# Attention after a recurrent layer, fp32: the row maxima of a unit are turned earlier, and two engines read a step's scores in opposite order

## The chip, the cores and the metric

One core of a Trainium2 chip. Its engines each work through a queue of their own in order: TensorE (PE in the profile, with its weight loads as PEld), VectorE (DVE), ScalarE (ACT), GpSimd (POOL) and SyncE (SP, for DMAs). The metric is the device time of one execution in microseconds (us). The kernel before takes 1719.53 us, the median of three runs (1718.27 to 1722.62).

## The reference

The input `x` is 2 x 2048 x 256, all in fp32. A layer norm and a tanh recurrence come first; their result is added to `x`. Then comes an attention layer with 8 heads of width 64, over 2048 queries and keys in each of the two batches, whose values and output go through gated experts:

```python
q = (x @ Wq).reshape(b, t, h, dh).transpose(0, 2, 1, 3)
k = (x @ Wk).reshape(b, t, h, dh).transpose(0, 2, 1, 3)
v = jnp.einsum('bthe,btek->bhtk', wv, xv)          # wv: top 2 of 5 gates, xv: 5 experts
scores = jnp.einsum('bhid,bhjd->bhij', q * scale, k)
probs = jax.nn.softmax(scores, axis=-1)
attn = jnp.einsum('bhij,bhjd->bihd', probs, v)
out = jnp.einsum('bthe,bthk,ekd->btd', mask_o, attn, Wo)
```

The softmax is what the change is about: each query needs the largest of its 2048 scores before any exponential can be taken.

## The kernel before

The first 180 us (recurrence, norms, the first batch's gates and experts) are not touched. The attention is 16 heads (2 batches x 8) of four **units** each: a unit is one head and one block of 512 queries, 64 units in all. Scores are held turned, keys on the partitions. A unit has eight **pairs** of key blocks; a pair is 2 x 128 keys by 512 queries, a tile of 128 x 1024. The main loop (L864) takes one **step** T at a time, with two new pairs in each, so a unit takes four steps: T % 4 = 0 brings pairs 0 and 1, and T % 4 = 3 brings pairs 6 and 7. I call them steps 0 to 3. `manual_schedule` keeps the order in which the code issues; there is no planner.

For a new pair `scores` (L497) issues matmuls into a PSUM tile `s`, of which there are two (`ps_s`, bufs=2), so a pair's tile is written again one step later, when all of its readers are done. `stage` (L512) has ScalarE copy it to SBUF, into `p`. `largest` (L517) has VectorE take the running maximum `m` (L525); pair 0 is not read for this, since pair 1 is compared with pair 0's copy. The last pair of the unit is handled in halves (L528 to L531), which gives `mm`, one maximum per partition and query. Where ScalarE and VectorE read the same PSUM tile, the framework orders the two reads as the code has them.

In step 0 of the next unit these maxima are turned: `turn_max` (L534) transposes `mm` on TensorE into `pm`, `reduce_max` (L541) has VectorE take the maximum along the row (`mq`, L543), and `spread_max` (L545) broadcasts and transposes it back into `pt` (L553), of which ScalarE makes a copy `top` in SBUF (L556). In step 1 pairs 0 and 1 have the maximum subtracted on VectorE, from `pt` in PSUM (`subtract`, L558 and L563); pairs 2 to 7 follow in steps 2, 3 and 0 on GpSimd, from `top`. ScalarE takes the exponential in place (L566). A step later `products` (L568) multiplies by the values into `o`; `fold` (L585) adds pairs with GpSimd DMAs and `sums` (L590) forms the denominators `d` with matmuls, in odd steps.

Other work hangs in two tables of steps: `before` runs ahead of a step's products, `behind` at its end. In step 0 `behind` holds `close` of an older unit, registered ahead of the newer unit's `spread_max`. `close` transposes that unit's result into `po` on TensorE (`weigh`, L629), and has VectorE form the denominators and gates (`den` L631, L635, L638) and the masked product `pro` (L642). At step 2 `take` (L608) reads `o` with ScalarE and then VectorE (`os`, L613); at step 3 `take_sums` does so for `d` (L619, L620). `keys` and `queries` of the next head stand in step 2 of three units of four, and in step 3 of one. `mix` (L488, `xq`) and `mix_sum` (L494) form the values in steps 2 and 3. Small PSUM tiles (`pm`, `pt`, `po`, `pk`, `pq`, `pv`, `pgl`, `py`, `pz`, `mh`) share two buffers (`misc`, L401).

Of the kernel before, what the change touches and what calls it, by code (L numbers as in the profile page):

```python
# [20 lines left out]
def rnn_then_switchhead_kernel(  # L21
# [16 lines left out]
    B, T, D = x.shape  # L38
# [20 lines left out]
    for c in range(NCH):  # L59
        t = rconst.tile([P, B, D], F32, tag=f"x{c}", name=f"x{c}")  # L60
# [258 lines left out]
    with tc.tile_pool(name="rnn", bufs=2) as rp, tc.tile_pool(  # L319
# [7 lines left out]
        for g in range(2):  # L327
            mv = rp.tile([P, GC, 2], F32, tag="mv", name=f"mvb{g}")
            for k in range(GC):
                c = g * GC + k  # L330
# [10 lines left out]
            for k in range(0, GC, 2):  # L341
                c = g * GC + k
# [25 lines left out]
            for k in range(GC):  # L368
                c = g * GC + k
# [22 lines left out]
    U_T = NCH // 4  # L392
# [8 lines left out]
    def misc(shape, nm):  # L401
        return ps_m.tile(shape, F32, tag="m", name=nm)
# [3 lines left out]
    NT = len(units) * U_T  # L406
    k_of, v_of, q_of, xq_of, y_of = {}, {}, {}, {}, {}
    ring, m_of, mm_of, mx_of, top_of, o_of, den_of = {}, {}, {}, {}, {}, {}, {}
    HC = NCH // 2
# [24 lines left out]
    def queries(i, part):  # L434

        b, h = heads[i]
        pq = misc([P, QB], f"pq{i}_{part}")
        for kc in range(KC):
            for o in range(2):
                n = 2 * part + o  # L440
                for g in range(0, DH, 32):
                    at_col = o * DH + g
                    nc.tensor.matmul(  # L443
                        pq[at_col : at_col + 32, :],
                        lhsT=wq[:, kc, h * DH + g : h * DH + g + 32],
                        rhs=xn2T[:, kc, b, n * QB : (n + 1) * QB],
                        start=kc == 0,
                        stop=kc == KC - 1,
                        tile_position=(0, at_col),
                    )  # L450
        q = ap.tile([P, QB], F32, tag="q", name=f"q{i}_{part}")
        qs = ap.tile([P, QB], F32, tag="qs", name=f"qs{i}_{part}")
        nc.scalar.mul(q, pq, SCALE)
        nc.sync.dma_start(out=qs[0:DH, :], in_=q[DH:P, :])
        nc.sync.dma_start(out=qs[DH:P, :], in_=q[0:DH, :])
        q_of[i, 2 * part] = (q, qs)
        q_of[i, 2 * part + 1] = (qs, q)
# [39 lines left out]
    def scores(t):  # L497
        i, n = units[t // HC]
        c = t % HC
        ss = ps_s.tile([P, 2, QB], F32, tag="s", name=f"s{t}")  # L500
        for o in range(2):
            half = slice(o * DH, (o + 1) * DH)
            nc.tensor.matmul(  # L503
                ss[:, o, :],
                lhsT=k_of[i][half, c, :],
                rhs=q_of[i, n][o][half, :],
                start=True,
                stop=True,
            )
        return ss  # L510

    def stage(t, ss):  # L512
        p = ap.tile([P, 2, QB], F32, tag=f"p{t % 2}", bufs=RING[t % 2], name=f"p{t}")
        nc.scalar.copy(p, ss)  # L514
        ring[t] = p

    def largest(t, ss):  # L517
        u, c = t // HC, t % HC
        if c == 0:
            return  # L520
        if c == 1:
            m_of[u] = ap.tile([P, 2, QB], F32, tag="mx", bufs=1, name=f"m{u}")
        m = m_of[u]
        if c < HC - 1:
            nc.vector.tensor_tensor(m, ss, ring[t - 1] if c == 1 else m, ALU.max)  # L525
            return
        half = misc([P, QB], f"mh{u}")
        nc.vector.tensor_tensor(half, ss[:, 0, :], m[:, 0, :], ALU.max)  # L528
        nc.vector.tensor_tensor(m[:, 1, :], ss[:, 1, :], m[:, 1, :], ALU.max)
        mm_of[u] = ap.tile([P, QB], F32, tag="mm", bufs=1, name=f"mm{u}")  # L530
        nc.vector.tensor_tensor(mm_of[u], half, m[:, 1, :], ALU.max)  # L531
        m_of.pop(u)

    def turn_max(u):  # L534
        pm = misc([P, QS, P], f"pm{u}")
        mm = mm_of.pop(u)
        for s in range(QS):
            nc.tensor.transpose(pm[:, s, :], mm[:, s * P : (s + 1) * P], ident)
        mx_of[u] = (pm, ap.tile([P, QS], F32, tag="mq", name=f"mq{u}"))

    def reduce_max(u):  # L541
        pm, mq = mx_of[u]
        nc.vector.tensor_reduce(mq, pm, AX.X, ALU.max)  # L543
# [14 lines left out]
    def subtract(t):  # L558
        u, c = t // HC, t % HC
        p = ring[t]  # L560
        last = u == len(units) - 1 and c % 2 == 0
        eng, top = (nc.vector, top_of[u][0]) if c < 2 or last else (nc.gpsimd, top_of[u][1])
        eng.tensor_tensor(p, p, top.unsqueeze(1).to_broadcast([P, 2, QB]), ALU.subtract)  # L563

    def exponential(t):
        nc.scalar.activation(ring[t], ring[t], AF.Exp)  # L566
# [18 lines left out]
    def fold(t):  # L585


        nc.gpsimd.dma_start(out=ring[t], in_=ring.pop(t + 1), accum_op=ALU.add)  # L588
# [19 lines left out]
    def take(u):  # L608

        o = o_of.pop(u)  # L610
        os = ap.tile([P, QB], F32, tag="os", bufs=1, name=f"os{u}")
        nc.scalar.copy(os[0:DH, :], o[0:DH, :])
        nc.vector.tensor_tensor(os[0:DH, :], o[DH:P, :], os[0:DH, :], ALU.add)  # L613
        o_of["s", u] = os
# [159 lines left out]
        late["c"].pop(0)()  # L774


    before, behind = {}, {}

    def at(table, T, f, *a):
        table.setdefault(T, []).append(lambda: f(*a))  # L780
# [5 lines left out]
    for i, (b, h) in enumerate(heads):  # L786
# [8 lines left out]
        for part in range(4):  # L795
            if i == 0:
                T = LAG - 3 + part
# [3 lines left out]
            else:  # L801
                T = max(T0 + U_T * (part - 3) + 2, LAG + 2)
# [6 lines left out]
    for b in range(1, B):  # L809

        T0 = (b - 1) * H * H_T + 2 * LAG + 3
        for c in range(NCH):
            T = T0 + c // 2 * U_T
# [6 lines left out]
        for c in range(NCH):  # L820
            T = T0 + 2 * c
# [12 lines left out]
    for u, (i, n) in enumerate(units):  # L834
        b, h = heads[i]
        T1 = (u + 1) * U_T
        at(before, T1, turn_max, u)
        at(before, T1, reduce_max, u)
        at(behind, T1, spread_max, u)
        outs = [(b, n * QS + s) for s in range(QS)]  # L840
        if u == len(units) - 1:

            outs = [(b, c) for c in range(n * QS - QS, n * QS + QS)]
            todo = [(turn_out, *outs[0])]
            for k, o in enumerate(outs):
                todo += [(turn_out, *x) for x in outs[k + 1 : k + 2]] + [(project_out, *o)]
            at(behind, T1 + LAG - 1, fetch_y, u)
            for x in todo[:3] + [(take_sums, u), (close_last, u)] + todo[3:]:
                at(behind, T1 + LAG, *x)
            continue  # L850
        at(behind, T1 + LAG + 1, take_sums, u)
        at(behind, T1 + LAG + 2, close, u)
        at(behind, T1 + LAG + 3, gather, u)
        if h == H - 1:
            at(behind, T1 + LAG, fetch_y, u)
            if u < len(units) - 2:
                for s in range(QS):
                    at(behind, T1 + LAG + 4 + s, turn_out, *outs[s])
                    at(behind, T1 + LAG + 5 + s, project_out, *outs[s])

    with tc.manual_schedule():
        queries(0, 0)
        keys(0, 0)
        for T in range(NT + LAG + 1):  # L864
            new = [t for t in (2 * T, 2 * T + 1) if T < NT]
            sub = [t for t in (2 * (T - LAG + 1), 2 * (T - LAG + 1) + 1) if 0 <= t < 2 * NT]
            old = [t for t in (2 * (T - LAG), 2 * (T - LAG) + 1) if 0 <= t < 2 * NT]
            u_old = (T - LAG) // U_T - 1
            done = (T - LAG) % U_T == 0 and 0 <= u_old < len(units)
            if done:  # L870
                take(u_old)
            if sub and sub[0] % HC == 0:
                subtract(sub[0])
            if old:
                exponential(old[1])
            for t in new:
                ss = scores(t)
                stage(t, ss)
                largest(t, ss)
            if sub and sub[0] % HC:  # L880
                subtract(sub[0])
            k = T - LAG
            if 0 < k < NT - U_T + 1:
                fold(2 * (k - 1))
            if sub:
                subtract(sub[1])
            for f in before.pop(T, []):
                f()
            for t in old:
                products(t)  # L890
            if 3 <= k and k % 2 and k - 3 < NT - U_T:
                t = 2 * (k - 3)
                sums(t, t + 2, t % HC == 0, t % HC != 0)
            if NT - 2 <= k < NT:

                t0 = 2 * (NT - U_T)
                for t in range(t0, t0 + 4, 2) if k == NT - 2 else ():
                    sums(t, t + 1, t == t0, False)
                sums(2 * k, 2 * k + 1, False, k == NT - 1)
            if sub:  # L900
                exponential(sub[0])
            for f in behind.pop(T, []):
                f()
        assert not before and not behind


# [44 lines left out]
```

## Time and profile before

| | |
|---|---|
| median of three runs | 1719.53 us |
| the profiled execution | 1725.14 us, span 1723.4 us |
| mean granted clock of TensorE | 0.982 |
| busy: PE, DVE, ACT, POOL | 91%, 76%, 71%, 73% |
| attention, from the first to the last score matmul | 178.6 to 1649.7 us |
| 1100 to 1640 us: busy PE, PEld, DVE, ACT, POOL | 512.5, 167.6, 457.5, 435.8, 464.3 of 540 us |
| pages' costliest groups: PE `s` (L503) | 2 x 526 us, 632 ns each |
| DVE maximum (L525) | 391.8 + 78.4 us, 1224 ns each |
| ACT copy (L514), exponential (L566) | 494.4 and 540.0 us, 1015 and 1066 ns each |
| POOL and DVE subtraction (L563) | 2996 and 1210 ns each |

A group row of the profile gives busy time, the mean duration of one instruction, and the idle time of the engine before it with what ended it. A wait row reads "who, line, waited for whom, line: us in total, times, longest". In a timeline row the first two numbers are start and duration, and x2 or x16 means that so many instructions are merged. Matmuls overlap, so their start-to-start distance counts, not their duration.

### The profile page before, as it was taken

The page shows a single profiled execution, that of the slowest core. Times are in us where ns is not written, and L with a number is a line of the kernel's source. Part 1 is how long each engine was busy: PE and PEld are TensorE (multiplying, and loading weights), DVE is VectorE, ACT ScalarE, POOL GpSimd, SP SyncE. Part 2 cuts the span into 40 slices and gives each one's busy share as a digit, 9 for nine tenths or more (in the row PEclk, how much of TensorE's full clock was granted, in tenths as well). Part 3 has the DMA queues.
Part 4 walks back from the last instruction along what each step waited for, and adds up shares of the span by engine and source line. Part 5 has one row for each costly group of instructions (what it writes and reads, how often), then busy time and mean ns, then how long its engine had stood idle before and what let it go on. Part 6 is the DMA issues. An engine that isn't in the chain of part 4 may idle for free.

```text
span 1723.4 us, 27125 instructions
## 1 busy us (share of the span) xinstructions
PE 1571.2 (91%) x10338; PEld 623.2 (36%) x10338; DVE 1312.7 (76%) x1861; ACT 1229.2 (71%) x1609; POOL 1264.5 (73%) x832
## 2 busy tenths in 40 slices
PE   6978689999989999999999999999999999999986
PEld 5976223232223333333323343333333333333234
DVE  5464588989887876678887668888888888888752
ACT  3642468787777887678887667787878787878861
POOL 3001667888778987679998757888888888888870
PEclk9998889999999999999999999999999999999999
DMA  4003157788777877678887656788888888888752
GB/s 152 1 34 116 54 132 175 174 181 171 153 155 159 165 159 162 153 154 161 166 174 161 153 133 164 167 160 169 162 170 161 169 162 169 162 168 182 150 121 80
DMA packets 88918, 254.74 MB, mean 148 GB/s; under 512 B 12176, under 2 KB 33488, under 8 KB 88784
## 3 DMA queue, kind: packets, MB, share of 16 engines
q0 software_dynamic: 43200, 163.60, 52.0%
q1 hardware_dynamic: 43952, 88.76, 16.1%
q8 instruction: 83, 1.36, 0.3%
q10 hardware_dynamic: 1632, 0.61, 0.1%
q14 instruction: 51, 0.42, 0.1%
HBM read 62.08 MB, written 50.33 MB: 65 GB/s over the span
## 4 chain that ended last, share of the span: by engine, by line
PE 49%; DVE 23%; ACT 11%; issue 5%; DMA 4%; POOL 1%; SPq 0%; ACTq 0%; DVEq 0%; POOLq 0%
PE s L503 20%; PE o L576 13%; DVE m L525 11%; ACT p L514 7%; PE d L597 4%; PE pq L443 3%; DVE p L563 3%; PE pt L553 2%; PE pk L424 2%; DVE mq L543 2%; DVE xq L488 2%; ACT p L566 2%; DVE v L494 1%; DMA p<-p 1%; PE pz L715 1%
## 5 line engine op out<-in xcount | busy, mean ns | idle before, releaser
L563 POOL TENSOR_TENSOR p<-p,top 128x1024 f32<-128x1024 f32 x381 | 1049.4, 2996 | 19.7 <-ACT top L556 19.7
L566 ACT ACTIVATE p<-p 128x1024 f32<-128x1024 f32 x512 | 540.0, 1066 | 79.2 <-DVE p L563 77.2
L503 PE MATMUL s<-qs,k 64*128 64x512 f32 x1024 | 525.9, 632 | 18.7 <-DVE m L525 18.4
L503 PE MATMUL s<-q,k 64*128 64x512 f32 x1024 | 526.1, 632 | 10.8 <-DVE m L525 10.1
L514 ACT COPY p<-s 128x1024 f32<-128x1024 f32 x512 | 494.4, 1015 | 20.7 <-PE s L503 17.4
L576 PE MATMUL o<-p,v 128*32 128x512 f32 x4096 | 493.1, 598 | 10.8 <-DVE os L613 7.5
L525 DVE TENSOR_TENSOR m<-s,m 128x1024 f32<-128x1024 f32 x320 | 391.8, 1224 | 136.5 <-ACT p L514 119.4
L588 POOL DMA_DIRECT2D p<-p x252 | 320.1, 1270 | 82.5 <-ACT p L514 35.5
L503 PEld LDWEIGHTS s<-qs,k 64*128 64x128 f32 x1024 | 173.0, 189 | 162.4 <-DVE m L525 86.3
L576 PEld LDWEIGHTS o<-p,v 128*32 128x32 f32 x4096 | 112.7, 109 | 315.6 <-issue 191.0
L503 PEld LDWEIGHTS s<-q,k 64*128 64x128 f32 x1024 | 172.9, 189 | 148.4 <-DVE m L525 70.1
L563 DVE TENSOR_TENSOR p<-p,pt 128x1024 f32<-128x1024 f32 x131 | 158.5, 1210 | 0.1
L525 DVE TENSOR_TENSOR m<-s,p 128x1024 f32<-128x1024 f32 x64 | 78.4, 1224 | 83.9 <-ACT p L514 83.5
L597 PE MATMUL d<-p,ones 128*32 128x512 f32 x1040 | 136.2, 592 | 0.7 <-DMA p<-p 0.7
L684 POOL DMA_DIRECT2D yd<-pro x48 | 42.3, 882 | 123.6 <-DVE pro L642 121.7
L556 ACT COPY top<-pt 128x512 f32<-128x512 f32 x64 | 37.5, 586 | 107.8 <-PE pt L553 107.8
L488 DVE TENSOR_TENSOR xq<-xq,wp 128x1280 f32<-128x1280 f32 x64 | 95.1, 1487 | 10.0 <-DMA xq<-xvd 8.0
L642 DVE TENSOR_TENSOR pro<-po,mr 128x1280 f32<-128x1280 f32 (+1 forms) x67 | 95.9, 1431 | 2.7
L494 DVE TENSOR_REDUCE v<-xq 128x256 f32<-128x1280 f32 x64 | 94.5, 1476 | 0.1
L156 POOL TENSOR_SCALAR xn<-x,mb,zb 128x256 f32<-128x256 f32 x8 | 5.2, 656 | 107.8 <-DVE zb L146 90.9
L553 PE MATMUL pt<-ident,mq 128*128 128x128 f32 x256 | 42.3, 289 | 43.1 <-DVE mq L543 42.4
L443 PE MATMUL pq<-xn2T,wq 128*32 128x512 f32 x512 | 61.6, 598 | 5.7 <-DVE xq L488 4.6
(139 smaller groups left out, 1544.7 us busy)
## 6 DMA issues: line engine op xcount, KB each, us to landing
p<-p POOLq DMA_DIRECT2D x252, 512.0 KB, 5.7
xq<-xvd SPq DMA_DIRECT2D x64, 640.0 KB, 6.2
yd<-pro POOLq DMA_DIRECT2D x48, 640.0 KB, 6.8
qs<-q SPq DMA_DIRECT2D x64, 128.0 KB, 2.3
yd<-pro SPq DMA_DIRECT2D x8, 640.0 KB, 3.8
y<-yd SPq DMA_DIRECT2D x8, 640.0 KB, 6.1
x<-in_x SPq DMA_DIRECT2D x16, 256.0 KB, 5.5
x1d<-x SPq DMA_DIRECT2D x16, 256.0 KB, 2.0
```

The lines of the kernel that those rows point to most:

```text
L443: nc.tensor.matmul(pq[at_col : at_col + 32, :], lhsT=wq[:, kc, h * DH + g : h * DH + g + 32], rhs=xn2T[:, kc, b, n * QB : (n + 1) * QB], s ...
L488: nc.vector.tensor_tensor(xq, xq, wp.unsqueeze(2).to_broadcast([P, 4, DH, E]), ALU.mult)
L494: nc.vector.tensor_reduce(v_of[i][:, 4 * part : 4 * part + 4, :], xq, AX.X, ALU.add)
L503: nc.tensor.matmul(ss[:, o, :], lhsT=k_of[i][half, c, :], rhs=q_of[i, n][o][half, :], start=True, stop=True,)
L514: nc.scalar.copy(p, ss)
L525: nc.vector.tensor_tensor(m, ss, ring[t - 1] if c == 1 else m, ALU.max)
L563: eng.tensor_tensor(p, p, top.unsqueeze(1).to_broadcast([P, 2, QB]), ALU.subtract)
L566: nc.scalar.activation(ring[t], ring[t], AF.Exp)
L576: nc.tensor.matmul(o_of[u][at_col : at_col + 32, :], lhsT=v_of[i][:, 2 * c + o, g : g + 32], rhs=ring[t][:, o, :], start=c == 0, stop=c == ...
L588: nc.gpsimd.dma_start(out=ring[t], in_=ring.pop(t + 1), accum_op=ALU.add)
L597: nc.tensor.matmul(den_of[u][32 * g : 32 * (g + 1), :], lhsT=ones32, rhs=ring[(t, t1)[g // 2]][:, g % 2, :], start=first, stop=last, tile_ ...
L642: nc.vector.tensor_tensor(dst, po[:, s : s + n, 0:DH].unsqueeze(2).to_broadcast([P, n, E, DH]), mr[:, s : s + n].unsqueeze(3).to_broadcast ...
```

## The change

Three things change in the order in which a step issues; no instruction is added or removed.

In steps 0, `turn_max` and `reduce_max` are issued ahead of the step's own maximum instead of in the table `before`, and `spread_max` goes to a table of its own, `first_behind`, which runs ahead of all that is in `behind`. In steps 1 to 3 the two engines begin with different pairs: ScalarE copies the first pair and then the second, VectorE takes the maximum of the second pair and then of the first; the half-wise handling moves from the last pair to the last but one. In step 1 the second subtraction on VectorE stands between the two maxima, where it was behind both.

```diff
     def largest(t, ss):
         u, c = t // HC, t % HC
-        if c == 0:
-            return
...
-        if c < HC - 1:
+        if c != HC - 2:
             nc.vector.tensor_tensor(m, ss, ring[t - 1] if c == 1 else m, ALU.max)
             return
...
-        at(before, T1, turn_max, u)
-        at(before, T1, reduce_max, u)
-        at(behind, T1, spread_max, u)
+        at(first_behind, T1, spread_max, u)
...
-            if sub and sub[0] % HC == 0:
+            fresh = sub and sub[0] % HC == 0
...
+            if fresh:
                 subtract(sub[0])
             if old:
                 exponential(old[1])
-            for t in new:
-                ss = scores(t)
-                stage(t, ss)
-                largest(t, ss)
-            if sub and sub[0] % HC:
+
+            ss = [scores(t) for t in new]
+            if new:
+                stage(new[0], ss[0])
+            if T % U_T == 0:
+                if new:
+                    stage(new[1], ss[1])
+                if 0 < T <= NT:
+                    turn_max(T // U_T - 1)
+                    reduce_max(T // U_T - 1)
+                if new:
+                    largest(new[1], ss[1])
+            elif new:
+                largest(new[1], ss[1])
+                stage(new[1], ss[1])
+            if fresh:
+                subtract(sub[1])
+            if T % U_T and new:
+                largest(new[0], ss[0])
+            if sub and not fresh:
                 subtract(sub[0])
             k = T - LAG
             if 0 < k < NT - U_T + 1:
                 fold(2 * (k - 1))
-            if sub:
+            if sub and not fresh:
                 subtract(sub[1])
...
-            for f in behind.pop(T, []):
+            for f in first_behind.pop(T, []) + behind.pop(T, []):
                 f()
```

More of the change, by code (lines that the diff above doesn't have):

```diff
@@ L774, in gates_go_on @@
         late["c"].pop(0)()
-    before, behind = {}, {}
+    before, first_behind, behind = {}, {}, {}
     def at(table, T, f, *a):
@@ L864, in rnn_then_switchhead_kernel @@
         for T in range(NT + LAG + 1):
-            new = [t for t in (2 * T, 2 * T + 1) if T < NT]
+            new = (2 * T, 2 * T + 1) if T < NT else ()
             sub = [t for t in (2 * (T - LAG + 1), 2 * (T - LAG + 1) + 1) if 0 <= t < 2 * NT]
@@ L901, in rnn_then_switchhead_kernel @@
                 exponential(sub[0])
-            for f in behind.pop(T, []):
+            for f in first_behind.pop(T, []) + behind.pop(T, []):
                 f()
-        assert not before and not behind
+        assert not before and not behind and not first_behind
 def kernel(
```

## The prediction

> **What bounds the kernel now.** I read the page first, then the granted clock (0.982, so nothing is explained by it), then the waits of 1100 to 1640 us, where the kernel only repeats itself, and last the timelines of one unit there.
>
> ```profile
> PE 1571.2 (91%) x10338; PEld 623.2 (36%) x10338; DVE 1312.7 (76%) x1861; ACT 1229.2 (71%) x1609; POOL 1264.5 (73%) x832
> ```
>
> TensorE is busy 91% of the span, in 1100 to 1640 even 512.5 of 540 us. The 27.5 us that are left there, some 5%, are nearly all in four waits (us in total, times, longest):
>
> ```profile
> PEld s L503 <- DVE m L525: 69.0, 100, 1.5
> DVE m L525 <- ACT p L514: 63.9, 52, 2.4
> ...
> ACT p L566 <- DVE p L563: 35.6, 25, 1.4
> ...
> PE pt L553 <- DVE mq L543: 16.8, 26, 0.7
> ...
> PE s L503 <- DVE m L525: 5.6, 14, 0.6
> ...
> PE o L576 <- DVE os L613: 3.0, 7, 0.4
> ...
> PE pq L443 <- DVE xq L488: 2.4, 6, 0.4
> ```
>
> The PE rows, 16.8 + 5.6 + 3.0 + 2.4 = 27.8 us, are idle time of TensorE; the PEld rows are weight loads, which run beside matmuls and cost nothing by themselves. The wait that comes once in every unit is `pt` on `mq`, 0.65 us. DVE's wait for ACT's copy, and ACT's for DVE's subtraction, lie on engines with idle time. Here is that place on TensorE (start, duration):
>
> ```profile
> 1312.90 0.65 PE L538 MATMUL pm<-ident,mm 128*128 128x128 f32 x4
> 1313.48 1.92 PE L576 MATMUL o<-p,v 128*32 128x512 f32 x16
> 1315.34 0.66 PE L629 MATMUL po<-ident,os 128*128 128x128 f32 x4
> 1316.64 0.65 PE L553 MATMUL pt<-ident,mq 128*128 128x128 f32 x4 [0.65 <-DVE mq L543]
> 1317.22 0.69 PE L503 MATMUL s<-q,k 64*128 64x512 f32 x1
> ...
> 1321.85 0.69 PE L503 MATMUL s<-q,k 64*128 64x512 f32 x1
> ```
>
> and on VectorE:
>
> ```profile
> 1314.77 1.23 DVE L525 TENSOR_TENSOR m<-s,p 128x1024 f32<-128x1024 f32 x1 [0.59 <-ACT p L514]
> 1315.91 0.68 DVE L543 TENSOR_REDUCE mq<-pm 128x4 f32<-128x512 f32 x1
> 1316.50 0.16 DVE L631 TENSOR_REDUCE den<-po 128x4 f32<-128x8 f32 x1
> ...
> 1317.13 1.49 DVE L642 TENSOR_TENSOR pro<-po,mr 128x1280 f32<-128x1280 f32 x1
> 1318.54 1.21 DVE L563 TENSOR_TENSOR p<-p,pt 128x1024 f32<-128x1024 f32 x1
> 1319.81 2.56 DVE L525 TENSOR_TENSOR m<-s,m 128x1024 f32<-128x1024 f32 x2
> 1322.28 1.21 DVE L563 TENSOR_TENSOR p<-p,pt 128x1024 f32<-128x1024 f32 x1
> ```
>
> I count a step from the first matmul of its scores. Step 0 (T divisible by 4) starts at 1310.98, step 1 at 1317.22, step 2 at 1321.85, then 1327.34 and 1331.97: lengths 6.24, 4.63, 5.49, 4.63, together 20.99 us per unit. The reader is to see two things. TensorE has no gap but the 0.65. And in step 1 VectorE is the engine with a backlog: it comes to step 1 with `pro` and two subtractions to do beside the two maxima. It still frees the first pair's buffer in time: the first maximum ends 1.235 us after 1319.81, at S1 + 3.82 (S1 is the start of step 1), and TensorE comes back to that buffer at S1 + 4.63. The cover is 0.8 us.
>
> **Part 1: turned maxima ahead.** `mq` no longer stands behind the maximum at 1314.77, which waits for ScalarE. VectorE is done with `os` (L620) at 1314.18 and `pm` at 1313.55, so `mq` runs from about 1314.2 to 1314.9; `o` ends its issue at 1315.34, where `pt` now follows at once. The 0.65 us goes. The maximum starts at 1314.9 rather than 1314.77, which nobody waits for. Step 0 on TensorE is then 1.92 (scores) + 0.58 (`pm`) + 1.86 (`o`) + 0.58 (`pt`) + about 0.66 (`po`, by its own row) = 5.60, against 6.24. But `spread_max` now stands in a list that runs ahead of `close`, so `pt` is ahead of `po`, and `po` is the last thing in step 0. It ends about 0.08 after S1, and `den` follows 0.04 later (units at 995 to 1030 us show 0.04 from `po` to `den`): `den` at S1 + 0.12, where it was at S1 - 0.72. So what VectorE still has to do comes later against S1, not earlier. ScalarE's `top` comes 0.6 us earlier, which POOL's subtractions don't wait for here.
>
> **Part 2: different pairs first, and the second subtraction between the maxima.** In step 1 VectorE's queue was `pro`, subtract, max of pair one, max of pair two, subtract. Now it is `pro`, subtract, max of pair two, subtract, max of pair one. From start to start, by the rows above: `den` to `pro` 0.63, `pro` to subtract 1.41, subtract to max 1.27, max to subtract 1.24, subtract to max 1.27, and 1.23 for the last: 7.05 us. From S1 + 0.12 the first pair's buffer comes free at S1 + 7.17, and TensorE needs about 0.05 after a release (at 1347.79 after a maximum ending at 1347.74): step 2 starts at **S1 + 7.22, not at S1 + 4.63**. Nothing else on TensorE can fill this: the scores are the first matmuls of step 2, and both steps' products stand behind or are done. This is the new wait, +2.59 us. All its instructions are in the trace in these shapes, and VectorE's maximum beside ScalarE's copy of the other pair is seen there at the same 1.23, so I give the rows no margin. Pair two's buffer is freed at S1 + 4.7 by VectorE, then by ScalarE's copy 1.0 later, early enough.
>
> In steps 2 and 3 VectorE gains: it starts with pair two as soon as it is scored (1.97 + 0.03 after the step's start) and needs not wait for ScalarE's exponential and copy, for which it idled 1.30. Both maxima are done at S2 + 4.47. With 1.74 us of keys or queries in step 2 TensorE needs 5.49 anyway: gain 0. In the one unit in four without them step 2 was 4.94 and step 3 5.10 (waits of 0.43, 0.60 and 0.20); they become about 4.50 and 4.66, a gain of 0.88. In the unit with queries in step 3 the 0.40 behind `xq` goes (6.82 to 6.42). In step 3 the first pair is freed by `mh` and `m` at S3 + 4.66: 0.03 lost, as that max comes second. ScalarE's 1.43 before its exponential goes; this shortens no chain that TensorE waits for.
>
> **The sum.** Ordinary units: 5.60 + 7.22 + 5.49 + 4.66 = 22.97 against 20.99, +1.98 (two of four); 21.98 against 20.91, +1.07 (no keys or queries); 24.73 against 23.18, +1.55. The 27 such units from 1053 to 1632 us give 13 x 1.98 + 8 x 1.07 + 6 x 1.55 = 43.6 us. Sixteen units (257 to 453 and 779 to 935 us) have statistics or gate work on VectorE and a step 0 of up to 6.81; this work stands ahead of `mq`, so I put their step 0 at 5.75 to 5.90. From 196.2 and 156.1 us they go to about 210.1 and 165.6: +23.4. Twenty units (the first three, 453 to 779 and 935 to 1053 us) have other work on TensorE: in five of them step 1 was 5.0 to 5.1, which gives +2.0 each; in fifteen it was 4.0 to 7.1 with step 0 at 5 to 9, where the new wait is mostly covered, and I take +0.7 each (0 to 2). Together 20 us. Sum 43.6 + 23.4 + 20 = **+87 us**. The profiled execution took 1725.1 us (span 1723.4) and would take 1812; the median of the runs is 5.6 us lower, so 1807.
>
> One rule speaks against this. The Trainium skill, in "Perfetto Trace Analysis", section "Identifying the Most-Contended Engine", says that matmul busy time is a poor measure of how full TensorE is and that the share of weight loading is a better one. In 1100 to 1640 that share is 167.6 of 540 us, 31%; by it TensorE would have room to make up a late start, and the change would come out near 1720. The rows decide: steps without a wait repeat at 4.63 and 5.49 to 0.01 us, with 0.43 between starts in every group of matmuls, so lost time is not made up.
>
> **Rivals.** (1) *The wait does not form; only the old ones go.* Decided by whether pair one's buffer is free by S1 + 4.58; my chain misses that by 2.6 us. It would need `po` and `den` about that much earlier, or `pro` and a subtraction out of the way. Then TensorE's idle time from 230 to 1690 us goes: at `pt` 40.0, scores 14.6, `o` behind `os` 7.5, `pq` 4.6, at most 67; with what ends each of them changed, 40 to 67: 1653 to 1680. For it: the three waits that the edits aim at are real rows. Against: the order of five instructions on one in-order queue.
> (2) *A smaller loss.* If `po` ran ahead of `pt`, or VectorE were ahead by `pro` (2.04 us from `den` to the subtraction), the wait would be 0.5 us, less the 0.65: about 0 to +1 per unit, 1720 to 1775. The code's lists speak against it.
> (3) *A larger loss.* `pt` now holds one of the two small PSUM buffers while everything else of step 0 must pass through the other. At 556.35 `po` started 0.04 after the copy of `pgl` ended, and 0.6 before the reader of `pm` did, so a buffer is taken as it comes free; now the twenty fuller units would run `pv` or `pz`, a copy, `py`, a copy and `po` one behind the other. One to two us more in each: +20 to +35, 1827 to 1842.
>
> **How the numbers follow.** Forecast (1780 to 1826) 0.73; larger loss 0.09; smaller loss 0.08, of which 0.02 within 0.3%; faster 0.10, of which 0.01 within 0.3%. About 0.3% is what a measurement of this kernel can tell from no change. So faster 0.09, same 0.03, slower 0.88. The range leaves out the faster side and the ends of the others: 1765 to 1835.
>
> **What would show it.** Right: `pt`'s wait on `mq` is gone; `PE s <- DVE m` becomes the largest idle row of TensorE, some 2.5 us per unit, always at the start of step 2; step 1 is 7.2 us long, step 0 5.6; `den` follows `po` by 0.04 in all units; ScalarE's wait for DVE's subtraction is nearly gone. Wrong: step 1 still 4.63, or `po` ahead of `pt`.

## The result, and the profile after

The changed kernel takes 1720.59 us (median; 1717.95 to 1723.96), the kernel before 1720.18 us (1718.27 to 1722.62) in the runs beside it. The ratio is 1.0003 with a 95% interval of 0.9996 to 1.001: no change. The forecast of 1807 was 86 us too high. The profiled execution after took 1720.86 us, span 1719.1 at a granted clock of 0.983. In the changed kernel the lines of the functions named here have numbers smaller by one from the maximum on (maximum L524, subtraction L562, `po` L628).

The page's first row and three of its groups (busy, mean ns of one | idle before, and what ended it):

```profile
PE 1571.3 (91%) x10338; PEld 622.5 (36%) x10338; DVE 1312.4 (76%) x1861; ACT 1233.9 (72%) x1609; POOL 1261.5 (73%) x832
...
L514 ACT COPY p<-s 128x1024 f32<-128x1024 f32 x512 | 511.1, 1011 | 261.8 <-DVE m L524 136.3
L503 PE MATMUL s<-qs,k 64*128 64x512 f32 x1024 | 529.5, 630 | 40.8 <-ACT p L514 39.4
L503 PE MATMUL s<-q,k 64*128 64x512 f32 x1024 | 529.8, 630 | 29.0 <-ACT p L514 27.3
```

TensorE has the same work and nearly the same idle time. The scores wait for ScalarE's copy; the forecast had them wait for VectorE's maximum. ScalarE idles 261.8 us ahead of its copies, where it idled 20.7 before; 136.3 of it is for VectorE's read of the same tile. All waits of TensorE in 1100 to 1640 us of the kernel after:

```profile
PE s L503 <- ACT p L514: 24.1, 30, 0.9
PE d L596 <- DMA p<-p: 0.8, 1, 0.8
```

The four rows of before (16.8 + 5.6 + 3.0 + 2.4 = 27.8 us) are gone, `pt` on `mq` among them, and one row of 24.1 us stands in their place. From 230 to 1690 us, all idle time of TensorE counted, the sums are 86.7 us before and 83.4 after.

One step 0 and step 1 on TensorE, in the same unit as in the prediction (start, duration, idle before):

```profile
1311.24 0.65 PE L552 MATMUL pt<-ident,mq 128*128 128x128 f32 x4
1311.73 0.60 PE L628 MATMUL po<-ident,os 128*128 128x128 f32 x4
1312.26 0.69 PE L503 MATMUL s<-q,k 64*128 64x512 f32 x1
...
1315.92 1.04 PE L596 MATMUL d<-p,ones 128*32 128x512 f32 x8
1317.90 0.69 PE L503 MATMUL s<-q,k 64*128 64x512 f32 x1 [0.94 <-ACT p L514]
...
1319.07 0.69 PE L503 MATMUL s<-q,k 64*128 64x512 f32 x1
```

The same stretch on VectorE, and ScalarE's copy of pair two:

```profile
1311.23 1.23 DVE L524 TENSOR_TENSOR m<-s,p 128x1024 f32<-128x1024 f32 x1 [0.77 <-ACT p L514]
1312.37 0.16 DVE L630 TENSOR_REDUCE den<-po 128x4 f32<-128x8 f32 x1
...
1313.00 1.49 DVE L641 TENSOR_TENSOR pro<-po,mr 128x1280 f32<-128x1280 f32 x1
1314.41 1.21 DVE L562 TENSOR_TENSOR p<-p,pt 128x1024 f32<-128x1024 f32 x1
1315.54 1.22 DVE L524 TENSOR_TENSOR m<-s,m 128x1024 f32<-128x1024 f32 x1
1316.67 1.21 DVE L562 TENSOR_TENSOR p<-p,pt 128x1024 f32<-128x1024 f32 x1
1317.80 1.22 DVE L524 TENSOR_TENSOR m<-s,m 128x1024 f32<-128x1024 f32 x1
```

```profile
1316.83 1.01 ACT L514 COPY p<-s 128x1024 f32<-128x1024 f32 x1 [2.34 <-issue]
```

Here is what the forecast missed. Step 1 starts at S1 = 1312.26. The maximum of pair one, the last of VectorE's five, runs from 1317.80 to 1319.02, nearly where the forecast had it. But TensorE has begun step 2 at 1317.90, **before this maximum is done**: 0.06 us after ScalarE's copy of pair *two* ended at 1317.84. It took pair two's buffer first, and needed pair one's only for its second scores, at 1319.07.

Steps, from first score matmul to first score matmul, 1100 to 1640 us:

| step | ordinary unit: before, forecast, after | no keys or queries | queries in step 3 |
|---|---|---|---|
| 0 | 6.24, 5.60, 5.38 | 6.24, 5.38 after | 6.24, 5.38 after |
| 1 | 4.63, 7.22, 5.64 | 4.63, 5.64 after | 4.63, 5.64 after (5.71 to 6.45 in three of six) |
| 2 | 5.49, 5.49, 5.80 | 4.94, 4.72 after | 5.49, 5.80 after |
| 3 | 4.63, 4.66, 4.63 | 5.10, 4.63 after | 6.82, 6.35 after |
| sum | 20.99, 22.97, 21.45 | 20.91, 20.36 after | 23.18, 23.17 after |

So +0.46, -0.55 and -0.01 us per unit. In the ordinary unit a gain of 0.86 in step 0 stands against losses of 1.01 and 0.31 in steps 1 and 2; over the 27 units of the repeating part 1.9 us are lost.

### The profile page after: what moved, and what is told of

Read it like the earlier page. It is cut to its first block, busy times and chain, and to the rows that moved or that the text cites. A ratio compares the mean times of both kernels' runs of the same rounds, so it can differ in the third digit from the quotient of the medians.

```text
span 1719.1 us, 27059 instructions
## 1 busy us (share of the span) xinstructions
PE 1571.3 (91%) x10338; PEld 622.5 (36%) x10338; DVE 1312.4 (76%) x1861; ACT 1233.9 (72%) x1609; POOL 1261.5 (73%) x832
## 3 DMA queue, kind: packets, MB, share of 16 engines
q10 hardware_dynamic: 1632, 0.61, 0.1%
## 4 chain that ended last, share of the span: by engine, by line
PE 53%; DVE 17%; ACT 9%; issue 8%; DMA 5%; POOL 1%; SPq 0%; ACTq 0%; DVEq 0%; POOLq 0%
PE s L503 20%; PE o L575 14%; DVE m L524 7%; ACT p L514 7%; PE d L596 4%; PE pq L443 3%; PE pk L424 3%; DMA p<-p 3%; DVE p L562 2%; PE pz L714 2%; ACT p L565 1%; DVE v L494 1%; DMA xq<-xvd 1%; PE pxv L372 1%; PE po L628 1%
## 5 line engine op out<-in xcount | busy, mean ns | idle before, releaser
L562 POOL TENSOR_TENSOR p<-p,top 128x1024 f32<-128x1024 f32 x381 | 1036.6, 2910 | 7.1 <-ACT top L555 7.0
L514 ACT COPY p<-s 128x1024 f32<-128x1024 f32 x512 | 511.1, 1011 | 261.8 <-DVE m L524 136.3
L524 DVE TENSOR_TENSOR m<-s,m 128x1024 f32<-128x1024 f32 x320 | 390.8, 1221 | 98.0 <-PE s L503 87.4
L587 POOL DMA_DIRECT2D p<-p x252 | 298.2, 1183 | 82.1 <-ACT p L514 27.1
L503 PEld LDWEIGHTS s<-qs,k 64*128 64x128 f32 x1024 | 169.4, 188 | 189.0 <-ACT p L514 86.9
L503 PEld LDWEIGHTS s<-q,k 64*128 64x128 f32 x1024 | 169.4, 188 | 174.2 <-ACT p L514 75.2
L562 DVE TENSOR_TENSOR p<-p,pt 128x1024 f32<-128x1024 f32 x131 | 158.3, 1209 | 0.1
L596 PE MATMUL d<-p,ones 128*32 128x512 f32 x1040 | 143.9, 593 | 3.6 <-DMA p<-p 3.4
L524 DVE TENSOR_TENSOR m<-s,p 128x1024 f32<-128x1024 f32 x64 | 78.4, 1224 | 48.4 <-ACT p L514 48.2
L596 PEld LDWEIGHTS d<-p,ones 128*32 128x32 f32 x1040 | 35.2, 110 | 88.9 <-issue 77.3
L542 DVE TENSOR_REDUCE mq<-pm 128x4 f32<-128x512 f32 x64 | 44.3, 692 | 23.9 <-PE pm L537 22.2
```

The costliest lines, as they stand in the source:

```text
L503: nc.tensor.matmul(ss[:, o, :], lhsT=k_of[i][half, c, :], rhs=q_of[i, n][o][half, :], start=True, stop=True,)
L596: nc.tensor.matmul(den_of[u][32 * g : 32 * (g + 1), :], lhsT=ones32, rhs=ring[(t, t1)[g // 2]][:, g % 2, :], start=first, stop=last, tile_ ...
```

## The experiments

My theory after the result: the pool does not hand its two score buffers out in turn. A new tile gets the one whose readers come free first in the program, which is settled when the kernel is built. In the built instruction list of after, the first scores of step 2 wait on ScalarE and the second on VectorE; in before both wait on VectorE. In the same list of after, the first pair of steps 2, 3 and 0 lies in the PSUM bank of the second pair of the step ahead, in every unit; in before it never does. The rivals: the chain of the forecast was wrong in itself, or the three edits cancel for another reason.

Where units are counted, 0 is the first. Units 36 to 62 are the repeating part (about 1053 to 1632 us); the others have statistics, gates, experts or values beside them and are the fuller ones. Stretches in us, from one profiled execution each (`before` and `before_fixed`, whose steps are the same, differ by 1.7 us in 32-35 and by 0.1 in the others):

| kernel | median us | 3-11 | 15-19 | 20-23 | 32-35 | 36-62 |
|---|---|---|---|---|---|---|
| before | 1720.18 | 196.2 | 113.9 | 112.4 | 117.5 | 579.3 |
| after | 1720.59 | 196.8 | 116.6 | 112.3 | 114.4 | 581.2 |
| fixed_pairs | 1811.91 | 213.4 | 126.1 | 114.9 | 117.0 | 623.9 |
| before_fixed | 1721.33 | 196.2 | 113.8 | 112.4 | 115.8 | 579.2 |
| crossed_pairs | 1723.23 | 197.2 | 116.9 | 112.4 | 114.4 | 583.3 |
| turn_only | 1721.06 | 195.7 | 113.8 | 115.9 | 121.2 | 573.7 |
| swap_only | 1728.75 | 195.7 | 114.7 | 111.9 | 113.1 | 585.7 |
| between_only | 1721.10 | 197.9 | 115.7 | 110.0 | 115.7 | 581.5 |
| sub_behind | 1719.71 | 195.2 | 115.4 | 115.5 | 119.1 | 573.5 |
| after_pt_last | 1701.39 | 195.4 | 112.2 | 107.6 | 109.9 | 578.7 |
| turn_pt_last | 1695.29 | 194.3 | 112.1 | 110.9 | 114.7 | 563.2 |
| mixed | 1682.36 | 189.8 | 109.8 | 110.4 | 112.7 | 563.9 |

### Buffers by name: fixed_pairs, before_fixed, crossed_pairs

`fixed_pairs` is after, with one named buffer for the first pair of a step and one for the second; `before_fixed` is the same edit in before.

```diff
-        ss = ps_s.tile([P, 2, QB], F32, tag="s", name=f"s{t}")
+        ss = ps_s.tile([P, 2, QB], F32, tag=f"s{t % 2}", bufs=1, name=f"s{t}")
...
-            pt = ps_s.tile([P, 2, QB], F32, tag="s", name=f"pt{u}")[:, 0, :]
+            pt = ps_s.tile([P, 2, QB], F32, tag="s0", bufs=1, name=f"pt{u}")[:, 0, :]
```

The second line concerns the last unit alone, whose `pt` takes a score buffer. Expected of `fixed_pairs`:

> The changed kernel, but the two PSUM buffers of the scores have a name each, so that a step's first pair always goes into the buffer of the first pair before, and the second into that of the second. Theory (the pool gives the next pair whichever buffer is released first, and in the changed kernel that is the second pair's, by ScalarE's late copy): now the first scores of step 2 must wait for the last maximum of step 1, which ends 6.77 us after the step's start in the changed kernel, so step 1 grows from 5.64 to about 6.83 us, step 2 shrinks from 5.80 to 5.49, a unit of 21.44 us becomes about 22.3, and the whole 1755 to 1775 us, near what was forecast. Rival (the buffers alternate anyway and VectorE's chain was only shorter than worked out): no change, 1717 to 1724 us, step 1 at 5.64.

Measured: 1811.91 us (1810.46 to 1813.48), 1.0519 of before [1.0495, 1.0543]. The wait of the forecast is there, in TensorE's timeline and in its waits (1100 to 1700 us):

```profile
1194.17 1.04 PE L596 MATMUL d<-p,ones 128*32 128x512 f32 x8
1197.41 0.99 PE L503 MATMUL s<-q,k 64*128 64x512 f32 x1 [2.20 <-DVE m L524]
1197.42 1.05 PE L503 MATMUL s<-qs,k 64*128 64x512 f32 x1
1198.20 1.06 PE L503 MATMUL s<-q,k 64*128 64x512 f32 x1
```

```profile
PE s L503 <- DVE m L524: 58.2, 27, 2.2
```

One wait of 2.2 us on VectorE's maximum stands in each of the 27 units, against 0.94 on ScalarE. Step 1 is 6.90 us, against 5.64: the pool's choice is worth 1.26 us per unit in this step. The loss is larger than the expected 1755 to 1775, and most of the excess is what follows some of these waits: the matmuls from 1197.41 last 1.05 us and stand 0.8 apart, where in the kernel after they last 0.59 and stand 0.42 apart. Here are two neighbouring stretches around this wait, and two around the wait of 2.20 us that ended at 1317.47 (length; busy of PE, PEld, DVE, ACT, POOL; granted clock; DMA share; GB/s):

```profile
1194.21:1197.62 3.41, 1.21 (x14) 0.33 (x8) 3.13 (x4) 2.54 (x4) 3.41 (x3) 1.00 1.05 172
1197.62:1201.04 3.42, 3.42 (x12) 1.02 (x14) 0.62 (x1) 1.87 (x2) 3.42 (x2) 0.50 0.96 189
1313.68:1317.09 3.41, 1.58 (x16) 0.26 (x8) 3.41 (x4) 1.95 (x3) 3.41 (x4) 1.00 1.08 171
1317.09:1320.51 3.42, 3.04 (x20) 1.19 (x24) 1.94 (x3) 2.45 (x4) 3.42 (x3) 1.00 1.03 207
```

Behind the first wait the granted clock falls from 1.00 to 0.50 for 3.4 us, behind the second it does not. Where it falls, step 2 takes 7.13 us, not 5.49. This happens behind 18 waits of 2.2 us in the whole attention, which makes some 30 us (18 x 1.64). Which of them it is, the last section shows.

Expected of `before_fixed`:

> The kernel before with a PSUM buffer of its own for each of the two pairs of a step. Theory (the pool hands out the buffer released first; before the change the first pair is always released first, so the buffers alternate by themselves): nothing changes, 1717 to 1725 us, unit of 20.99 us. Rival (a name for each buffer costs time by itself, which would take the verdict from the same edit on the changed kernel): over 1740 us.

Measured: 1721.33 us, 0.9994 [0.9983, 1.0004], with the step lengths of before. Naming the buffers costs nothing where the order of release is the order of the pairs, so the 91 us between `fixed_pairs` and after come from the buffers' exchange and what follows from it.

`crossed_pairs` names the buffers too, but exchanges them in steps 2 and 3:

```diff
+        cross = (t // 2) % U_T >= 2
+        ss = ps_s.tile([P, 2, QB], F32, tag=f"s{(t + cross) % 2}", bufs=1, name=f"s{t}")
...
```

> The changed kernel with a name for each of the two PSUM buffers of the scores, as in the run with fixed buffers, but with the two names exchanged in steps 2 and 3, so that the first pair of step 2 goes into the buffer of step 1's second pair by order of the code. Theory (this exchange is what the pool does in the changed kernel, and all that kept the forecast wait away): as the changed kernel, 1717 to 1726 us, step 1 at 5.64, no stretch of half the clock in the repeating part. Rival (the loss with fixed buffers came from naming the buffers, or from something other than which buffer the next pair gets): 1760 us or more.

Measured: 1723.23 us (1722.33 to 1723.95), 1.0002 [0.9993, 1.0011], steps 5.38, 5.64, 5.80, 4.63 in an ordinary unit. These are the steps of after, with the exchange written out by hand. One step differs: without keys and queries step 2 is 5.05 us, not 4.72. The pool of after exchanges the buffers at the start of step 3 too, and this edit does not. The theory of the buffers stands.

### The edits one by one: turn_only, swap_only, between_only, sub_behind

`turn_only` has the first edit alone: after, with the pairs in their old order on both engines and the second subtraction behind both maxima.

```diff
-        if c != HC - 2:
+        if c < HC - 1:
...
-            if new:
-                stage(new[0], ss[0])
...
+                    stage(new[0], ss[0])
...
             elif new:
-                largest(new[1], ss[1])
-                stage(new[1], ss[1])
-            if fresh:
-                subtract(sub[1])
-            if T % U_T and new:
-                largest(new[0], ss[0])
+                for t, s_ in zip(new, ss):
+                    stage(t, s_)
+                    largest(t, s_)
...
-            if sub and not fresh:
+            if sub:
                 subtract(sub[1])
```

> The first part alone: maxima turned ahead, their broadcast ahead of the other work of the step; both engines read the first pair first and the second subtraction stands behind both maxima, as in the kernel before. Theory: step 0 is 5.38 us as in the changed kernel (6.24 before). VectorE's chain begins at S1 + 0.11, so the first pair's buffer is free at about S1 + 4.6, just in time, the second pair's at about S1 + 5.8 where 5.6 is needed; ScalarE waits for the late subtraction, so step 2 and 3 lose some of it. About 0.3 us less per unit: 1695 to 1712 us, step 1 at 4.6 to 4.8. Rival (what is won at the turned maxima is always given back at the next buffer): 1716 to 1724 us, with a wait of 0.6 to 0.9 us at the scores of step 2.

Measured: 1721.06 us (1715.09 to 1724.25), 0.9988 [0.9975, 1.0]. The total missed the expected range and lies in the rival's. Step 0 is 5.38 and step 1 4.63, as expected. But of the 0.86 us gained in step 0 an ordinary unit gives 0.61 back: step 2 is 5.88 and step 3 4.85, where they were 5.49 and 4.63. The repeating part gains 5.6 us, some 0.2 per unit where 0.3 was expected, and this is lost in the fuller units, +3.5 in units 20 to 23 and +3.7 in 32 to 35. Two of TensorE's waits in 640 to 1050 us:

```profile
PE py L698 <- DVE p L562: 3.8, 4, 1.0
PE tpl L750 <- DVE p L562: 3.6, 3, 1.2
```

`py` and `tpl` use the two small PSUM buffers, and wait for the subtraction that is the last reader of `pt`. These two rows are 7.4 us together; in before they are 3.1. So the rival is right in part: the next buffers take back most of step 0's gain, the scores' in the repeating part and the small ones in the fuller units.

`swap_only` is before, with VectorE's second pair first in steps 1 to 3 and nothing else.

```diff
-        if c < HC - 1:
+        if c != HC - 2:
...
-            for t in new:
-                ss = scores(t)
-                stage(t, ss)
-                largest(t, ss)
+            ss = [scores(t) for t in new]
+            if new:
+                stage(new[0], ss[0])
+                if T % U_T:
+                    largest(new[1], ss[1])
+                stage(new[1], ss[1])
+                if T % U_T:
+                    largest(new[0], ss[0])
+                else:
+                    largest(new[1], ss[1])
```

> The kernel before with one edit: in steps 1 to 3 VectorE takes the second pair's maximum first. Turned maxima and the subtraction stay where they were. Theory: VectorE's chain begins at S1 - 0.72 as before; both buffers come free at S1 + 4.8 to 4.9, so step 1 grows from 4.63 to about 4.8 us, and VectorE no longer idles 1.30 us in step 2, which takes 0.4 to 0.9 us off the unit without keys and queries; the wait at the turned maxima stays at 0.65. About -0.1 us per unit: 1705 to 1720 us. Rival (ScalarE's second copy, now behind a maximum, delays the next exponentials and products): slower, 1725 to 1750 us.

Measured: 1728.75 us (1721.36 to 1731.9), 1.0035 [1.0019, 1.005]. Missed, on the side of the rival and in its range. Its waits on TensorE, 1100 to 1640 us:

```profile
PE pt L553 <- DVE mq L543: 26.9, 25, 1.2
PE s L503 <- ACT p L514: 2.9, 7, 0.4
PE o L576 <- DVE os L613: 1.1, 7, 0.2
```

The small waits shrink, but `pt` waits 26.9 us where before had 16.8, up to 1.21 in a unit where it was 0.65. ScalarE's copies of steps 2 and 3 now come behind VectorE's read of the same tile, and so does what follows them on ScalarE. In step 0 VectorE's maximum, which needs ScalarE's copy of pair 0, waits 1.50 us (0.59 before), and `mq` stands behind it in this kernel, so step 0 grows to 6.81 us in three units of four. Without the first edit the second one costs time.

`between_only` is before, with the second subtraction between the maxima.

```diff
                 largest(t, ss)
...
+                if fresh and t == new[0]:
+                    subtract(sub[1])
...
-            if sub:
+            if sub and not (fresh and new):
                 subtract(sub[1])
```

> The kernel before with one edit: in step 1 VectorE's second subtraction stands between the two maxima (first pair's maximum first). Theory: the first pair's buffer is free at S1 + 3.8 as before, the second pair's only at about S1 + 6.2 where TensorE wants it at 5.6, so the second scores of step 2 wait about 0.6 us; ScalarE's wait of 1.4 us for the subtraction goes, which gives 0.4 to 0.9 back in the unit without keys and queries. 0 to +0.5 us per unit: 1718 to 1745 us. Rival (freeing ScalarE is worth as much as the maxima cost): 1700 to 1716 us.

Measured: 1721.10 us, 0.9996 [0.9986, 1.0007]; steps 6.24, 4.63, 6.12, 4.63. Step 2 of an ordinary unit loses 0.63 us, and the unit without keys and queries gains 1.00 (19.91 against 20.91): nothing is left in the total, which is in the expected range. `sub_behind` is the opposite, after without its third edit:

```diff
-            if fresh:
-                subtract(sub[1])
             if T % U_T and new:
                 largest(new[0], ss[0])
...
-            if sub and not fresh:
+            if sub:
                 subtract(sub[1])
```

> The changed kernel with its third edit taken back: in step 1 the second subtraction stands behind both maxima again. Theory: step 1 keeps its 5.64 us, since what ends it, ScalarE's copy of the second pair, comes behind the first maximum as before; the first pair's maximum ends 1.13 us earlier, so the second scores of step 2 need not wait and step 2 shrinks from 5.80 to 5.49 us in three units of four: 1704 to 1714 us. Rival (the late subtraction delays ScalarE's exponential and with it the copies of step 2, which is what the edit was made against): 1720 us or more.

Measured: 1719.71 us (1716.89 to 1722.43), 0.9989 [0.998, 0.9998]. The steps are the expected ones, 5.38, 5.64, 5.49, 4.63, and the repeating part gains 7.7 us on after. The total was missed. Units 20 to 23 lose 3.2 and 32 to 35 lose 4.7, and the rows of `py` and `tpl` behind the subtraction are again 7.4 us; in after they do not occur. So the third edit costs in the repeating part and pays in the fuller units, by these rows because it frees `pt`'s buffer earlier.

### Where `pt` stands: after_pt_last, turn_pt_last, mixed

If `pt`'s small buffer is what the fuller units wait for, `pt` should be issued last, as in before. `after_pt_last` is after with one word changed; `turn_pt_last` is `turn_only` with the same.

```diff
-        at(first_behind, T1, spread_max, u)
+        at(behind, T1, spread_max, u)
```

> The changed kernel with one edit taken back: the broadcast of the maxima (pt) is issued behind the older unit's transposes (po) again. Theory (in the changed kernel VectorE's chain of step 1 starts late because po is the last thing on TensorE in step 0): den starts about 0.35 us ahead of step 1 instead of 0.11 behind it, step 1 shrinks from 5.64 to about 5.15 us, a unit of 21.44 to about 20.9, the whole 1685 to 1702 us. Rival (the order of the two transposes does not matter, VectorE is held by the maximum of step 0): 1715 to 1724 us, step 1 at 5.6.

Measured: 1701.39 us (1701.01 to 1703.02), 0.9884 [0.9868, 0.9899], in the expected range, though not where expected. In the repeating part only one unit in four has a step 1 of 5.20, the others stay at 5.63. `po` is now ahead, and `den` still late, by TensorE's and VectorE's timelines of one such unit:

```profile
1121.32 0.66 PE L628 MATMUL po<-ident,os 128*128 128x128 f32 x4
1121.81 0.60 PE L552 MATMUL pt<-ident,mq 128*128 128x128 f32 x4
1122.34 0.69 PE L503 MATMUL s<-q,k 64*128 64x512 f32 x1
```

```profile
1121.31 1.23 DVE L524 TENSOR_TENSOR m<-s,p 128x1024 f32<-128x1024 f32 x1 [0.77 <-ACT p L514]
1122.45 0.16 DVE L630 TENSOR_REDUCE den<-po 128x4 f32<-128x8 f32 x1
```

`po` is done at 1121.98, but `den` starts at S1 + 0.11 as in after, because step 0's maximum on VectorE, late behind ScalarE's copy, is ahead of it. That is the mechanism of the rival; its total was wrong. The gain is in the fuller units: 4.4 us in 15 to 19, 4.7 in 20 to 23, 4.5 in 32 to 35. In 640 to 1050 us TensorE's waits sum to 20.2 us in after and to 13.2 here. These rows of after are gone:

```profile
PE po L628 <- ACT yT L705: 2.7, 4, 0.7
PE py L698 <- DVE z L721: 2.1, 4, 0.5
PE po L628 <- ACT gates_all L763: 1.3, 4, 0.3
```

They are what the theory asks for: while `pt` holds one small buffer, `po` and `py` wait for the reader of the other.

> The kernel before with only this: the maxima are turned and reduced ahead of the step's own maximum. Order of the pairs, place of the second subtraction and place of pt as before. Theory: step 0 is 5.4 us (6.24 before), VectorE's chain starts about 0.35 us ahead of step 1, so both buffers are free in time (first pair at S1 + 4.1, second at S1 + 5.3 where 5.6 is needed) and nothing takes the place of the wait: about 0.6 us less per unit, 1680 to 1698 us. Rival (what is won is given back at the next buffer): 1714 to 1724 us.

Measured: 1695.29 us (1694.07 to 1696.63), 0.9847 [0.9833, 0.986], as expected. Steps 5.38, 4.63, 5.49 to 5.56, 4.80 to 4.85: of step 0's gain of 0.86 an ordinary unit keeps 0.6 to 0.7, since step 3 grows by some 0.2.

`mixed` adds to `turn_pt_last` the second pair first on VectorE in steps 2 and 3 alone. Seen from `after_pt_last`, step 1 has its old order back, and the second subtraction is behind both maxima as in `sub_behind`:

```diff
+            elif new and T % U_T == 1:
+                largest(new[0], ss[0])
+                stage(new[1], ss[1])
+                largest(new[1], ss[1])
             elif new:
                 largest(new[1], ss[1])
                 stage(new[1], ss[1])
-            if fresh:
-                subtract(sub[1])
-            if T % U_T and new:
                 largest(new[0], ss[0])
...
-            if sub and not fresh:
+            if sub:
                 subtract(sub[1])
```

> As the run with only the maxima turned ahead, and in steps 2 and 3, but not in step 1, VectorE takes the second pair first. Theory: step 1 stays at 4.63 us, and in steps 2 and 3 VectorE no longer waits for ScalarE's copy, which takes the waits out of the unit without keys and queries (step 2 of 4.94 to about 4.5, step 3 of 5.10 to 4.63) and the 0.40 us before queries: 0.1 to 0.3 us per unit below the run with only the turned maxima, 1668 to 1690 us. Rival (ScalarE's second copy, now late in steps 2 and 3, delays exponentials that the products need): no better than that run, or up to 15 us worse.

Measured: **1682.36 us** (1680.71 to 1684.7), 0.977 [0.9755, 0.9785], the fastest of all. The total is in the expected range, the place of the gain is not: the repeating part is level with `turn_pt_last` (563.9 and 563.2), and the gain is in units 3 to 11 (4.5 us), 15 to 19 (2.3) and 32 to 35 (2.0). What it is there stays open. TensorE's waits in 1100 to 1600 us:

```profile
PE o L575 <- DVE os L612: 4.0, 6, 0.7
PE s L503 <- ACT p L514: 3.1, 7, 0.6
PE d L596 <- DMA p<-p: 2.3, 3, 1.1
```

TensorE idles 9.4 us of 500 by these rows. But the rows understate one wait. Step 3 does shrink, to 4.63 us from 4.80 to 5.10 in `turn_pt_last` and to 6.35 from 7.07 with queries; step 2 without keys and queries is 5.44, where 4.5 was expected. And step 1 takes the gain back: in 13 of the 24 units from 39 to 62 it is 4.85 to 6.80 us, not 4.63, some 11 us in all. In each of the 13 the third of the eight matmuls of `d` starts 0.04 to 0.05 us after the folding DMA, which GpSimd issues, has landed; in `turn_pt_last` two units have this. GpSimd is busy 10.0 of 10.0 us from 1100 to 1110. That its load is what makes the DMA late is likely, and not tested.

## Why the prediction was wrong

**Part 1 was right on TensorE, and by luck on `den`.** `pt`'s wait on `mq` is gone in this stretch; `po` is last; `den` starts at S1 + 0.11, where S1 + 0.12 was forecast. But the forecast had step 0's maximum start some 1.7 us ahead of S1, with nothing waiting for it. It starts 1.03 ahead, held by ScalarE's copy, and alone would put `den`, which follows it by 1.14, at the same place: `after_pt_last`, with `po` ahead of `pt`, has S1 + 0.11 too. Step 0 is 5.38, not 5.60, since `pt` and `po` stand 0.49 and 0.53 from start to start and I took 0.58 and 0.66, which are rows with a wait or an end in them.

**Part 2 failed at "TensorE comes back to that buffer".** I had the buffers alternate and took the wait for pair one's, which is free last. In the kernel as built, the first scores of a step take the buffer that is free first, which in step 1 of the changed kernel is pair two's, so that only the second scores wait for VectorE's last maximum. `fixed_pairs` puts the assumption into the code and gets 6.90 for step 1; without it step 1 is 5.64. Of the 1.58 us that the forecast of 7.22 was too long, 1.26 is this. The remaining 0.32 is the 0.40 of the next point, less 0.09 by which TensorE starts later behind the release (0.14 us in `fixed_pairs`, 0.05 forecast). The evidence was in my own text: rival 3 noted that a small buffer "is taken as it comes free", and I did not put the same question to the score buffers.

**The chain on VectorE was right in order and too long by 0.4 us.** From `den` to the end of the last maximum it is 6.65 us (1312.37 to 1319.02), where 7.05 was forecast. The operations of 1.21 to 1.22 us stand 1.13 apart; my 1.24 and 1.27 came from pairs that had a wait between them or were merged in the row.

**Steps 2 and 3.** No gain of step 2 was forecast for ordinary units; it lost 0.31, since the second scores come 0.21 late and their first matmul takes 0.10 more to the next than in an unbroken group (0.53 and 0.43). The gains without keys and queries and of the 0.40 behind `xq` came, as 4.72 + 4.63 against a forecast 9.16, and 6.35 against 6.42.

**The sum.** In units 36 to 62 the forecast was +43.6 us, measured +1.9; `fixed_pairs` has +44.6. In units 3 to 11 it was 196.2 to 210.1; after has 196.8, `fixed_pairs` 213.4. So the forecast would have held for a kernel with named buffers, and its closeness there (1807 forecast, 1811.91 measured) is partly luck: step 1 is shorter than forecast, and the half clock, which I had not thought of, makes up for it (nine of its stretches, some 15 us, lie in units 36 to 62).

**The rivals.** Rival 2's lower end, 1720, holds the result, but not by its reasons: `pt` was ahead of `po` and VectorE no earlier. Rival 1 did not hold here; its mechanism is seen in part in `turn_pt_last` and `mixed`, where VectorE's order in step 1 is left alone. Rival 3 is real and was mis-sized for this kernel: the row of `py` and `tpl` grows from 3.1 to 7.4 us in `turn_only`, but the third edit takes it away again; `pt` ahead of `po` still costs 19.2 us in all (1720.59 against 1701.39).

**The rule that spoke against the forecast.** From the share of weight loading, which the Trainium skill, "Perfetto Trace Analysis", section "Identifying the Most-Contended Engine", puts in place of matmul busy time beside another measure, I had worked out that a late start would be made up, and the total did come out near 1720. It is not the reason: a wait of 2.20 us in place of 0.94 makes step 1 longer by 1.26 (6.90 and 5.64), the whole difference. What kept the total was less waiting, not time made up.

## What to carry to other kernels

Before counting when "the" buffer of a pool comes free, ask which of its buffers the next tile will get: list the last reader of each, in order, and take the earliest for the first tile; a named buffer each fixes the answer. Of two engines that read one tile the second sets its release, so an exchange of their order moves the release between engines, and puts work of the late engine behind it in the next steps too. A reordering that gains in the repeating part is counted in the fuller units as well, by how long each small shared buffer is held: here the three edits gain and lose some 3 to 8 us in one place or the other and cancel, while the first with `pt` left last, and the second without step 1, give 0.977.

## What the runs showed of the hardware

**The clock.** In `fixed_pairs` 18 of 44 waits of 2.2 us in the attention were followed by a granted clock of 0.50 for 3.41 us, some 1.6 us lost each (7.13 - 5.49). What separates the 18 from the other 26 is where they lie. In all twelve traces the granted clock changes only on a fixed grid of 3.41 us. In the four rows under `fixed_pairs` the first wait lies whole in one stretch of the grid, in which TensorE is busy 1.21 us; the second, 2.20 us as well, is divided by an edge into some 1.8 and 0.4. Each of the 18 waits has at least 2.05 us in one stretch, and none of the other 26 more than 1.97. Over all twelve traces, from 240 to 1700 us, each of the 68 falls of the clock came behind a stretch with 1.62 us or more idle, and no stretch at full clock with more than 1.97 us idle failed to be followed by one; in between both occur. Shorter waits count together: in `swap_only` the clock fell behind waits of 1.44 and 1.19 us, which ended 1.85 us apart, and behind none of 1.2 us that stood alone. The Trainium skill, "TensorE: Matmul & The Clock Gate", section "HAM oscillation — how this bites in real kernels", asks for no idle gaps above some 3.4 us; here some 2.05 us within one stretch of 3.41 were always enough.

**VectorE.** Two operations on 128 x 1024 with no wait between them overlap by 0.08 us (1.13 from start to start, 1.21 long). On a chain of five this is 0.3 to 0.4 us. Where the second needs the first's result, as with two maxima in a row, they stand 1.33 apart.
